# Group-norm attention on one core: the fp32 products for q and k in four column quarters of the array instead of two halves

## The chip, the cores and the metric

The kernel runs on one core of a Trainium2 chip. The metric is the device time of one launch in microseconds (us), lower is better. TensorE multiplies through a 128x128 array: a matmul holds a stationary operand (the weights; its rows are the contraction, its columns become output partitions in PSUM) and streams a moving operand of up to 512 columns past it. A matmul may use a part of the array only: 64 rows by 128 columns, 128 rows by 64 columns, and so on; matmuls on different parts can run beside each other. In the profile PE is the matmul side of TensorE and PEld its weight loads, DVE is VectorE, ACT ScalarE, POOL GpSimd, SP SyncE.

## The reference

```python
# x is (4, 512, 48, 48): b = 4 images, 512 channels, t = 2304 positions, 8 heads of d = 64
hn  = _group_norm(x, gn_scale, gn_bias)                       # 32 groups, fp32
qkv = einsum('oc,bchw->bohw', qkv_w, hn) + qkv_b              # fp32 product, 512 -> 1536 channels
qkv = qkv.reshape(b, 3, num_heads, d, t).astype(float16)
q, k, v = qkv[:, 0], qkv[:, 1], qkv[:, 2]
w = softmax(einsum('bhct,bhcs->bhts', q * scale, k * scale))
a = einsum('bhts,bhcs->bhct', w, v).astype(float32)
out = x + einsum('oc,bchw->bohw', proj_w, a) + proj_b
```

## The kernel before

The kernel has a fast path, which is what runs, and a fallback that a flag at the end would start. All sixteen pairs of heads (`g`, four in each image) go through the fast path one after the other. The positions are cut in five blocks (`QBLOCKS`, `j`): four of 512 and one of 256.

The work on TensorE has these parts. In brackets stand the part of the array that each uses, as rows x columns, and the line of the matmul:

- **scores** (64x128, L1134, tile `ps`): keys against queries in fp16, two heads at once, one in the upper and one in the lower 64 rows. ScalarE takes the exponential of the result (tile `p`, L1141).
- **values** (128x64, L1159, tile `av`): exponentials against v in fp16, one head in each 64 columns.
- **sums** (128x64, L1218, tile `sl`): exponentials against ones, at the end of each block.
- **v products** (128x64, L881, tile `pv`): normalised x against the v weights in fp32, two halves of 64 columns, 256 moving columns.
- **q and k products** (128x64, L829, tile `pqk`, in the opening `ps`, `first_av`, `first_w`): the q or k weights of a pair against normalised x in fp32, two halves of 64 columns, 512 or 256 moving columns. Each needs four channel chunks `c`, accumulated in one PSUM bank, which VectorE then empties into q or k (L840).
- **output projection** (128x128, L1019, tile `pr`).

The order on TensorE is fixed when the kernel is built. A list of steps (`stream`) has six to a block of 512 (three to the block of 256); a step issues the scores of three key tiles (or pairs of them), then fills in products that later pairs need, then the values of two steps before. `fill` takes those products from the list `beside`, in pieces: `chain_pieces` cuts a q or k chain of 512 columns in two pieces of two chunks each (`HALVES`) and leaves a chain of 256 whole. A step's pieces stand behind its values; in the step in which a block's sums are due, they stand between the sums and the values. The first 36 us hold the group norm of the first image with the first eight q and k chains. `idle_once` puts a no-op behind each of the first 190 matmuls of L829.

Of the kernel before, what the change touches and what calls it, by code (L numbers as in the profile page):

```python
# [23 lines left out]
HEADS, D = 8, 64  # L24
GROUP = C // 32
EPS = 1e-5
P = 128
# [448 lines left out]
def fast_path(  # L476
# [56 lines left out]
    wqkv = const.tile([P, NC, 3 * C], F32, name="wqkv")  # L533
# [93 lines left out]
    def chain_bank(name):  # L627
        if alone[0]:
            return ps_s.tile([P, 2, QB], F32, tag="ps", name=name)[:, 0, :]
        return ps_w.tile([P, QB], F32, tag="pw", name=name)  # L630
# [172 lines left out]
    def idle_once(*engines):  # L803
        for engine in engines:
            if idle_left[engine] > 0:
                idle_left[engine] -= 1
                getattr(nc, engine).nop("place", nofuse=True)
# [7 lines left out]
    def qk_steps(g, part, j, bank=None):  # L815
        b, pr = divmod(g, NPAIR)
        o, n = QBLOCKS[j]
        pw = {0: bank}

        def one(c):  # L820
            if g not in qk:
                qk[g] = [
                    qkp.tile([P, T], F16, tag=a, name=f"{a}_{g}") for a in ("q", "k")
                ]
            if c == 0 and bank is None:
                pw[0] = chain_bank(f"pqk_{g}_{part}_{j}")
            w0 = part * C + pr * P
            for lo in (0, D):
                nc.tensor.matmul(  # L829
                    pw[0][lo : lo + D, :n],  # L830
                    wqkv[:, c, w0 + lo : w0 + lo + D],
                    hn[b, c, j],
                    start=(c == 0),
                    stop=(c == NC - 1),
                )
                idle_once("tensor")

            def evacuate():
                col = part * NPAIR + pr
                nc.vector.tensor_scalar(  # L840
                    qk[g][part][:, o : o + n],
                    pw[0][:, :n],
                    bqkv[:, col : col + 1],
                    SCALE,
                    ALU.add,
                    ALU.mult,
                )

            if bank is not None:
                return evacuate  # L850
            if c == NC - 1:
                evacuate()

        return one
# [786 lines left out]
    n = QBLOCKS[j][1]  # L1641
# [141 lines left out]
```

## Time and profile before

| | before |
|---|---|
| median of 2 runs | 1588.49 us (1587.92 to 1589.07) |
| the profiled execution's own time | 1588.94 us |
| its span, first to last instruction | 1587.1 us |
| PE busy | 1572.5 us, 99% of the span |
| ACT busy | 1268.8 us, 80% |
| DVE busy | 1167.1 us, 74% |
| POOL busy | 319.3 us, 20% |
| mean granted TensorE clock | 0.998 |

The profile is of one execution. In a row of grouped instructions stand the line, the engine, the operation, what it writes and reads, the shapes and the count, then the busy time, the mean duration of one in ns and the idle time before them with what ended it. `128*64 128x512 f32` on a matmul is a stationary operand of 128 rows and 64 columns and a moving one of 512 columns. The ends of matmuls are modelled and overlap their successors, so the pace of TensorE is read from start to start. An fp32 matmul of the program shows as two weight loads and two matmuls in the trace; an fp16 one as one of each.

### The profile page before, as it was taken

To read this page: it belongs to the slowest core of one execution; us is meant where nothing else is said; L and a number is where in the kernel's file an instruction comes from. 1 tells how busy PE (TensorE), PEld (TensorE's weight loads), DVE (VectorE), ACT (ScalarE), POOL (GpSimd) and SP (SyncE) were. 2 spreads that over 40 slices of the span, in tenths; PEclk is the share of its full clock that TensorE was granted. 3 is DMA by queue.
4 is the path that set the end of the run, shared out by engine and by line. 5 is a ranking of instruction groups with operands and counts; after the bars stand their busy time and mean duration, and the time that the engine had idled before them with its cause. 6 is when DMAs were issued, how large, how long until landed. Compare 5 with 4: busy or idle time off the path is not lost. (4 is left out here: it accounts for less than half of the span.)

```text
span 1587.1 us, 28858 instructions
## 1 busy us (share of the span) xinstructions
PE 1572.5 (99%) x11526; PEld 678.0 (43%) x11526; DVE 1167.1 (74%) x1306; ACT 1268.8 (80%) x1363; POOL 319.3 (20%) x289
## 2 busy tenths in 40 slices
PE   9999999999999999999999999999999999999997
PEld 3733434443333543445333354344533334434543
DVE  6287678876766768987667766888767777777786
ACT  4177777888888888888888888888878888888995
POOL 1010201212212120311312231111122214131223
PEclk9999999999999999999999999999999999999999
DMA  7002120111212224621122222253022212215523
GB/s 226 1 21 78 48 75 27 31 57 48 68 42 63 68 58 121 170 81 42 51 67 57 56 63 68 85 173 101 12 67 64 68 48 65 68 48 175 163 70 128
DMA packets 115634, 119.87 MB, mean 76 GB/s; under 512 B 53156, under 2 KB 63268, under 8 KB 115492
## 3 DMA queue, kind: packets, MB, share of 16 engines
q1 hardware_dynamic: 113460, 116.11, 25.5%
q8 instruction: 92, 1.51, 0.4%
q10 hardware_dynamic: 1904, 1.84, 0.4%
q14 instruction: 50, 0.41, 0.1%
q0 software_dynamic: 128, 0.01, 0.0%
HBM read 79.58 MB, written 38.04 MB: 74 GB/s over the span
## 5 line engine op out<-in xcount | busy, mean ns | idle before, releaser
L1141 ACT ACTIVATE p<-ps 128x1024 f16<-128x1024 f32 x1296 | 1233.4, 1025 | 290.5 <-PE ps L1134 288.3
L1190 DVE TENSOR_TENSOR acc<-acc,p 128x3072 f16<-128x3072 f16 x270 | 495.7, 1836 | 51.9 <-ACT p L1141 49.4
L829 PE MATMUL pqk<-x,wqkv 128*64 128x512 f32 (+1 forms) x2432 | 510.3, 549 | 0.4 <-DVE k L840 0.3
L1159 PE MATMUL av<-p,v 128*64 128x512 f16 (+1 forms) x2880 | 360.7, 364 | 0.0
L1134 PE MATMUL ps<-q,k 64*128 64x512 f16 (+1 forms) x2880 | 356.1, 358 | 0.5 <-DVE v L889 0.2
L1286 POOL TENSOR_TENSOR att<-avx,ib 128x512 f16<-128x512 f32 (+1 forms) x78 | 123.1, 1578 | 1101.4 <-DMA ib<-row 835.3
L881 PE MATMUL pv<-wqkv,x 128*64 128x256 f32 x2304 | 267.6, 379 | 1.0 <-DVE v L889 1.0
L829 PEld LDWEIGHTS pqk<-x,wqkv 128*64 128x64 f32 x2432 | 168.6, 137 | 205.5 <-issue 155.8
L1134 PEld LDWEIGHTS <-k 64*128 64x128 f16 x2880 | 106.7, 94 | 287.8 <-issue 238.4
L1159 PEld LDWEIGHTS <-v 128*64 128x64 f16 x2880 | 131.4, 109 | 211.6 <-issue 167.0
L881 PEld LDWEIGHTS pv<-wqkv,x 128*64 128x64 f32 x2304 | 166.2, 137 | 82.5 <-DVE v L889 2.0
L1190 DVE TENSOR_TENSOR acc<-p,p 128x3072 f16<-128x3072 f16 x79 | 138.1, 1749 | 0.0
L1195 DVE TENSOR_TENSOR acc<-acc 128x1024 f16<-128x1024 f16 x156 | 134.7, 863 | 3.3
L953 POOL TENSOR_TENSOR pre<-pre,bproj 128x512 f32<-128x512 f32 x72 | 112.8, 1573 | 20.6 <-DMA pre<-x_dram 20.0
L889 DVE TENSOR_TENSOR v<-pv,bv 128x512 f16<-128x512 f32 x72 | 49.6, 690 | 77.7 <-PE pv L881 77.6
L840 DVE TENSOR_SCALAR q<-pqk,bqkv 128x512 f16<-128x512 f32 (+1 forms) x77 | 53.4, 693 | 70.9 <-PE pqk L829 70.6
L840 DVE TENSOR_SCALAR k<-pqk,bqkv 128x512 f16<-128x512 f32 (+1 forms) x75 | 52.1, 695 | 72.0 <-PE pqk L829 71.9
L1234 DVE COPY slx<-sl 128x512 f32<-128x512 f32 (+1 forms) x79 | 50.6, 641 | 62.4 <-PE sl L1218 62.4
L1019 PE MATMUL pr<-a,whi 128*128 128x512 f32 (+1 forms) x311 | 93.0, 418 | 0.0
L1041 DVE SCALAR_TENSOR_TENSOR r<-pr,r 128x512 f32<-128x512 f32 x75 | 51.5, 687 | 34.4 <-PE pr L1019 34.1
L1019 PE MATMUL pr<-att,wlo 128*128 128x512 f16 (+1 forms) x311 | 75.1, 361 | 0.6 <-DVE q L840 0.4
L1168 DVE COPY avx<-av 128x512 f32<-128x512 f32 (+1 forms) x79 | 50.4, 638 | 25.3 <-PE av L1159 25.2
(124 smaller groups left out, 456.5 us busy)
## 6 DMA issues: line engine op xcount, KB each, us to landing
pre<-x_dram SPq DMA_DIRECT2D x72, 256.0 KB, 3.1
xb<-pre SPq DMA_DIRECT2D x72, 256.0 KB, 3.3
r<-xb SPq DMA_DIRECT2D x72, 256.0 KB, 3.4
out_dram<-r SPq DMA_DIRECT2D x69, 256.0 KB, 2.6
ib<-row SPq DMA_DIRECT2D x126, 128.0 KB, 3.1
x<-x_dram SPq DMA_DIRECT2D x62, 256.0 KB, 4.2
x<-x_dram SPq DMA_DIRECT2D x16, 128.0 KB, 4.3
sums<-slx SPq DMA_DIRECT2D x128, 2.0 KB, 2.0
```

The source lines that it names most:

```text
L829: nc.tensor.matmul(pw[0][lo : lo + D, :n], wqkv[:, c, w0 + lo : w0 + lo + D], hn[b, c, j], start=(c == 0), stop=(c == NC - 1),)
L840: nc.vector.tensor_scalar(qk[g][part][:, o : o + n], pw[0][:, :n], bqkv[:, col : col + 1], SCALE, ALU.add, ALU.mult,)
L881: nc.tensor.matmul(pw[0][lo : lo + D, a, :], hn[b, c, i * P // QB][:, at + lo : at + lo + D], wqkv[:, c, 2 * C + half * C // 2 :][:, : C / ...
L953: nc.gpsimd.tensor_tensor(t, t, bias.to_broadcast(t.shape), ALU.add)
L1019: nc.tensor.matmul(ps[:, :n], w[:, bass.ts(m, P)], a, start=(i == 0), stop=(i == len(steps) - 1),)
L1041: nc.vector.scalar_tensor_tensor(xt, ps, DOWN, xt, ALU.mult, ALU.add)
L1134: nc.tensor.matmul(ps[:, h, a * n : (a + 1) * n], kt[rows, bass.ts(i, P)], qt[rows, o : o + n], start=True, stop=True,)
L1141: nc.scalar.activation(pt[:, r], ps, AF.Exp)
L1159: nc.tensor.matmul(av[0][lo : lo + D, :n], vv[b, pr // 2][:, i, pr % 2 * P + lo : pr % 2 * P + lo + D], pt[:, r, h, a * n : (a + 1) * n], ...
L1190: nc.vector.tensor_tensor(t, before, pt, ALU.add)
L1195: nc.vector.tensor_tensor(t[:, 0], t[:, 0], t[:, r], ALU.add)
L1286: nc.gpsimd.tensor_tensor(atts[g][:, o : o + n], avx.pop((g, j))[:, :n], ibs.pop((g, j))[:, :n], ALU.mult,)
```

## The change

Each q or k product of a chunk is now four matmuls of 32 columns, at the column positions 0, 32, 64 and 96, where it was two of 64. The sum over the chunks, the PSUM bank, the order of the pieces and all other engines' instructions stay as they are.

```diff
             w0 = part * C + pr * P
-            for lo in (0, D):
+            for lo in range(0, P, 32):
                 nc.tensor.matmul(
-                    pw[0][lo : lo + D, :n],
-                    wqkv[:, c, w0 + lo : w0 + lo + D],
+                    pw[0][lo : lo + 32, :n],
+                    wqkv[:, c, w0 + lo : w0 + lo + 32],
                     hn[b, c, j],
                     start=(c == 0),
                     stop=(c == NC - 1),
                 )
                 idle_once("tensor")
```

The first place is TensorE's order at an ordinary step of the first image: the values of an earlier step (`av`), half a q chain of the third pair (chunks 2 and 3, `x_2_1` and `x_3_1`), and the next scores. Of the program before:

```order
L1159 LDWEIGHTS v_0_517
L1159 MATMUL av_3_1504<-p_3_4_1552,v_0_517 64x512
L829 MATMUL pqk_0_1_1613<-x_2_1_129,wqkv 64x512 x2
L829 MATMUL pqk_0_1_1613<-x_3_1_139,wqkv 64x512 x2
L1134 LDWEIGHTS k_274
L1134 MATMUL ps_4_1_0_1662<-q_273,k_274 128x256
```

Of the changed program:

```order
L1159 LDWEIGHTS v_0_677
L1159 MATMUL av_3_1696<-p_3_4_1752,v_0_677 64x512
L829 MATMUL pqk_0_1_1821<-x_2_1_129,wqkv 32x512 x4
L829 MATMUL pqk_0_1_1821<-x_3_1_139,wqkv 32x512 x4
L1134 LDWEIGHTS k_274
L1134 MATMUL ps_4_1_0_1878<-q_273,k_274 128x256
```

Nothing moved; values and products were both 128x64 (written as 64 output partitions), and now a piece of 128x32 stands between the 128x64 values and the 64x128 scores. The second place is TensorE's order where a block ends: the sums (`sl`), half a q chain, then values. Of the program before:

```order
L1218 MATMUL sl_4_2915<-acc_4_2789,ones_160 64x256
L829 MATMUL pqk_0_3_2927<-x_0_3_111,wqkv 64x512 x2
L829 MATMUL pqk_0_3_2927<-x_1_3_123,wqkv 64x512 x2
L1159 LDWEIGHTS v_0_1854
L1159 MATMUL av_0_2933<-p_0_0_2824,v_0_1854 64x512
```

Of the changed program:

```order
L1218 MATMUL sl_4_3227<-acc_4_3093,ones_160 64x256
L829 MATMUL pqk_0_3_3239<-x_0_3_111,wqkv 32x512 x4
L829 MATMUL pqk_0_3_3239<-x_1_3_123,wqkv 32x512 x4
L1159 LDWEIGHTS v_0_2094
L1159 MATMUL av_0_3249<-p_0_0_3128,v_0_2094 64x512
```

Here, too, the order is the same, and the piece has 128x64 neighbours on both sides. Counted over the whole fast path, the neighbours of the q and k pieces on TensorE, the same in both programs, are:

| from | to | times | shape before | shape now |
|---|---|---|---|---|
| values | q/k | 198 | 64 to 64 columns | 64 to 32 |
| sums | q/k | 45 | 64 to 64 | 64 to 32 |
| q/k | values | 45 | 64 to 64 | 32 to 64 |
| q/k | v products | 1 | 64 to 64 | 32 to 64 |
| q/k | scores | 200 | 128x64 to 64x128 | 128x32 to 64x128 |
| scores | q/k | 2 | 64x128 to 128x64 | 64x128 to 128x32 |

TensorE changes the shape of the array part 954 times in the program before and 1243 times in the changed one. The matmuls of L829 go from 1280 to 2560, 4 of 5 with 512 moving columns and the rest with 256.

## The prediction

> **What bounds the kernel now.** I read the page first: its first line, the busy time of TensorE, and the strip of its busy tenths.
>
> ```profile
> span 1587.1 us, 28858 instructions
> PE 1572.5 (99%) x11526; PEld 678.0 (43%) x11526; DVE 1167.1 (74%) x1306; ACT 1268.8 (80%) x1363; POOL 319.3 (20%) x289
> PE   9999999999999999999999999999999999999997
> ```
>
> A busy 99% proves little on its own, because matmul ends are modelled. So I asked next what PE waited for; the columns are the total, the number of times and the longest wait in us.
>
> ```profile
> engine line waited for: us in total, times, longest us
> PE count L1722 <- DVE good L1721: 2.5, 1, 2.5
> PE idle L1482 <- DVE busy L1478: 1.5, 1, 1.5
> PE pv L881 <- DVE v L889: 1.0, 2, 0.9
> ```
>
> The two longest are the closing count and the opening; between them PE waits for about 1 us in all. TensorE is the bound from end to end, ScalarE and VectorE have a fifth and a quarter of the span to spare, and whatever TensorE gains or loses in the long middle reaches the end one for one. So the question is what a q or k piece costs on TensorE: its streaming, and its joints with the work before and behind it.
>
> **Streaming.** The first view is the timeline of PE at the end of a block, columns: start, length, engine, line, operation, names, shapes, count.
>
> ```profile
> 226.30 0.82 PE L1134 MATMUL ps<-q,k 64*128 64x512 f16 x6
> 227.05 0.41 PE L1218 MATMUL sl<-acc,ones 128*64 128x512 f16 x2
> 227.29 1.88 PE L829 MATMUL pqk<-x,wqkv 128*64 128x512 f32 x8
> 229.01 0.81 PE L1159 MATMUL av<-p,v 128*64 128x512 f16 x6
> 229.75 0.82 PE L1134 MATMUL ps<-q,k 64*128 64x512 f16 x6
> ```
>
> The lengths overlap; the pace is in the starts. The piece of two chunks has 8 records and hands over after 229.01 - 227.29 = 1.72 us. Records run in pairs, one in each half of the columns, so these are 4 rounds of **0.43 us**. An fp16 round of 512 takes half of that: the six values, three rounds, with a joint of 0.10 behind them (below), take 229.75 - 229.01 = 0.74, so (0.74 - 0.10) / 3 = 0.21. A 256-column fp32 round has its row here:
>
> ```profile
> 234.41 1.89 PE L829 MATMUL pqk<-x,wqkv 128*64 128x256 f32 x16
> 236.24 0.82 PE L1134 MATMUL ps<-q,k 64*128 64x512 f16 x6
> ```
>
> (1.83 - 0.10) / 8 rounds = 0.216 us. How many rounds there are follows from the counts of the line:
>
> ```profile
> L829 PE MATMUL pqk<-x,wqkv x2432: 379/592/643, 36.7 to 1440.1; 128*64 128x512 f32 x150, 128*64 128x256 f32 x38
> L829 PE MATMUL ps<-x,wqkv x96: 379/592/643, 10.7 to 34.6; 128*64 128x512 f32 x80, 128*64 128x256 f32 x16
> L829 PE MATMUL first_av<-x,wqkv x16: 592/592/593, 15.6 to 35.4; 128*64 128x512 f32 x16
> L829 PE MATMUL first_w<-x,wqkv x16: 592/592/593, 16.5 to 36.3; 128*64 128x512 f32 x16
> ```
>
> 2432 + 96 + 16 + 16 = 2560 records, two for each of the program's 1280 matmuls, are 1280 rounds, 1024 of 0.43 and 256 of 0.216: 440 + 55 = **495 us** of streaming on this line. Cut in quarters, a chunk has 4 matmuls with 2 records each. If all four quarters run at once, these are 2 rounds, as many as the halves need now, and a round streams the same 512 columns. The change removes nothing: it puts 4 x 32 columns where 2 x 64 filled the same 128. I take the streaming at no change. The bounds are wide, since no row shows four parts at work: if only two quarters ran at once, the rounds double, +495 us; if the two-fold length of an fp32 round came from the two halves hindering each other and vanished with narrow parts, a round could fall to the fp16 0.21, about -247 us. I choose nothing because the nearest rows, pairs of fp16 and of fp32 halves, each keep one steady pace.
>
> The added records must also be issued. With 256 columns a quartered round is 4 loads and 4 matmuls in 0.216 us, 27 ns each. The scores of the short block already run so:
>
> ```profile
> 161.85 0.83 PE L1134 MATMUL ps<-q,k 64*128 64x256 f16 x12
> 162.61 0.84 PE L1159 MATMUL av<-p,v 128*64 128x512 f16 x6
> ```
>
> 12 matmuls and as many loads in 0.76 - 0.10 = 0.66 us are 27 ns each, without a gap. So issue costs nothing; the no-ops that now end after half as many products fall away with it.
>
> **The joints.** Here the timeline of PE shows an ordinary step, and two steps in which the output projection follows the values:
>
> ```profile
> 215.62 0.84 PE L1159 MATMUL av<-p,v 128*64 128x512 f16 x6
> 216.29 1.88 PE L829 MATMUL pqk<-x,wqkv 128*64 128x512 f32 x8
> 218.10 0.82 PE L1134 MATMUL ps<-q,k 64*128 64x512 f16 x6
> ...
> 630.29 0.84 PE L1159 MATMUL av<-p,v 128*64 128x512 f16 x6
> 631.07 1.04 PE L1019 MATMUL pr<-att,wlo 128*128 128x512 f16 x4
> ...
> 633.72 0.84 PE L1159 MATMUL av<-p,v 128*64 128x512 f16 x6
> 634.49 1.04 PE L1019 MATMUL pr<-att,wlo 128*128 128x512 f16 x4
> ```
>
> The same six values, entered from scores each time, hand over to q/k after 0.67 us, and to the projection after 0.78 and 0.77. The products keep the shape 128x64; the projection goes to 128x128, with the rows unchanged. So a change of the columns alone costs **0.10 us**. The way out to the scores costs the same: 218.10 - 216.29 = 1.81 against the 1.72 of the block's end, where values of the same shape follow.
>
> A second, smaller price falls on the first round behind a change, since its weights can't be loaded under the work before. The six values take 0.74 to the scores at 229.01, where they follow products of their shape; entered from scores, with a joint behind, they take 0.77 (above): 0.03. For fp32 weights of 64 columns a row exists too:
>
> ```profile
> 76.84 1.94 PE L829 MATMUL pqk<-x,wqkv 128*64 128x512 f32 x8
> 78.71 1.11 PE L1134 MATMUL ps<-q,k 64*128 64x512 f16 x6
> ```
>
> This piece was entered from scores and takes 1.87, not 1.81: 0.06. No row has fp32 weights of 32 columns. They are half as wide, so I take half, 0.03; the bounds are 0 and 0.06. Four quarters that start one after another may cost something too. This row shows how an offset is paid:
>
> ```profile
> 104.58 0.85 PE L1159 MATMUL av<-p,v 128*64 128x512 f16 x6
> 105.37 0.82 PE L1134 MATMUL ps<-q,k 64*128 64x512 f16 x6
> ```
>
> Here six values behind a product take 0.79 instead of 0.74, because the two halves run apart until the next change of shape; 0.05 is my upper bound for that in an entry, and I take nothing.
>
> **The sum.** The order on TensorE gives 198 + 45 = 243 entries into a q/k piece from 128x64 work and 45 + 1 = 46 ways out into it; all 289 were free and become changes of shape. The 200 ways out to scores and the 2 entries from them are changes now and stay so. Each new one costs 0.10 and a first load of 0.03 (32 fp32 columns on the way in, 64 fp16 columns on the way out): 289 x 0.13 = **+37.6 us**. Against the profiled execution's 1588.94 (its span of 1587.1 and 1.8 around it; the median, 1588.49, is 0.03% lower) that is 1626.5. The lower bound leaves the joint alone, 289 x 0.10 = 28.9, so 1617.8; the upper takes 243 x (0.10 + 0.06 + 0.05) + 46 x 0.13 = 57.0, so 1646. Nothing on another engine hides this: VectorE and ScalarE wait for TensorE, and a longer TensorE only lengthens their waits. A longer run also moves no order, since that is fixed.
>
> **The rivals.**
>
> *No change of shape between 64 and 32 columns* (the other side). The 0.10 is seen where columns go from 64 to 128. If two column widths can follow each other without emptying the array, 289 times nothing remains, 1589, or up to 1596 with first loads in 243 entries at 0.03. It decides at 31.8 us (2%) over 289, or 0.11 us a joint: below, the kernel is not slower by over 2%. Against it: every change of shape in the rows, of rows or of columns, costs about 0.10. Chance 0.10.
>
> *Two quarters at a time.* The rounds double: 1588.9 + 37.6 + 495 = 2122. For it: nothing in this trace has more than two parts working at once. Against it: two parts keep their pace whatever they stream. Chance 0.08.
>
> *Four at once, but slower.* Four fp32 streams read twice what any row here reads at a time; if a round stretches, each per cent costs 5 us on top of 1626.5, anything from 1646 to 2122. Chance 0.07. The Trainium skill, in "TensorE: Matmul & The Clock Gate" (Measured speedup vs the span model), has three column tiles of 512 columns at 2.38 times, not 3. Taken as a rate, rounds would stretch by 3 / 2.38 = 1.26, an estimate of 1755 us. The halves here show no such loss, and nothing in this trace shows three or more.
>
> *A faster round.* If narrow parts run an fp32 round at the fp16 pace, 495 falls by 247: 1588.9 + 37.6 - 247 = 1379. For it, only that 0.43 is twice 0.21; against it, both records of a matmul take 0.43 steadily, with two streams of equal width to the fp16 case. Chance 0.04. The Trainium skill, "TensorEngine Tiling (Array Packing)" (Theoretical Speedup), gives up to 2 times for 64 and up to 4 times for 32 columns, which read as a promise is this rival. It speaks of a matrix that is small, and here four small ones make up the same 128 columns.
>
> That the change isn't in effect is no rival: the order shows 2560 matmuls of 32 columns.
>
> **How the numbers follow.** My forecast, four quarters at the old pace with 289 new changes of shape, has 0.71, and its own range is 1618 to 1646. To hold 8 in 10 the range takes in the case without a price for the change: 1589 to 1646, 0.81. Over 2% (about what a measurement of this kernel can tell from no change) begins at 1620.3. The forecast lies above it unless a joint costs under 0.11, which I give 0.10 of its 0.71. Slower: 0.61 + 0.08 + 0.07 = 0.76; within 2%: 0.10 + 0.10 = 0.20; faster: 0.04.
>
> **What would show it.** In the timeline of the changed kernel the starts from values to a q/k piece should lie 0.77 us apart, not 0.67; a two-chunk piece of 16 records should reach the scores after about 1.84, and from the sums to it there should be 0.34, not 0.24. If the first is 0.67, the joint is free; if the piece takes 3.5, only two run at once; if it takes 1.0, rounds got shorter. PE should still wait for about nobody, and ScalarE's idle time should grow by what the span does.

## The result, and the profile after

The changed kernel takes 1627.53 us (median of 2 runs, 1627.44 to 1627.62) against 1588.49 before: 1.0246 times as long, 95% interval 1.0202 to 1.029, or +39.0 us. The profiled execution took 1627.44 us with a span of 1625.6.

The head of its page, and the longest waits of PE (total us, times, longest):

```profile
span 1625.6 us, 33978 instructions
PE 1610.0 (99%) x14086; PEld 645.4 (40%) x14086; DVE 1167.4 (72%) x1306; ACT 1268.9 (78%) x1363; POOL 323.7 (20%) x289
```

```profile
PE count L1722 <- DVE good L1721: 2.5, 1, 2.5
PE idle L1482 <- DVE busy L1478: 1.5, 1, 1.5
PE first_means L729 <- DVE moments L655: 1.3, 1, 1.3
PE pv L881 <- DVE v L889: 1.0, 2, 0.9
```

The matmul records grew by 2560, the span by 38.5 us, and PE still waits for almost nobody. The 1.3 us at `first_means` lie in the opening, and the opening is no longer for it: the first q and k chain starts at 10.41 us, where it started at 10.74. VectorE and ScalarE have the same busy times as before; the exponentials' idle time went from 290.5 to 328.8 us in this group of the page, +38.3, which is the span's growth handed on. Before and after:

```profile
L1141 ACT ACTIVATE p<-ps 128x1024 f16<-128x1024 f32 x1296 | 1233.4, 1025 | 290.5 <-PE ps L1134 288.3
L1141 ACT ACTIVATE p<-ps 128x1024 f16<-128x1024 f32 x1296 | 1233.5, 1025 | 328.8 <-PE ps L1134 324.6
```

The timeline of PE in the changed kernel (start, length, engine, line, operation, names, shapes, count), first ordinary steps, then the end of a block:

```profile
219.50 0.84 PE L1159 MATMUL av<-p,v 128*64 128x512 f16 x6
220.27 1.93 PE L829 MATMUL pqk<-x,wqkv 128*32 128x512 f32 x16
222.12 0.82 PE L1134 MATMUL ps<-q,k 64*128 64x512 f16 x6
...
227.02 3.64 PE L829 MATMUL pqk<-x,wqkv 128*32 128x512 f32 x32
230.59 0.82 PE L1134 MATMUL ps<-q,k 64*128 64x512 f16 x6
231.35 0.41 PE L1218 MATMUL sl<-acc,ones 128*64 128x512 f16 x2
231.68 1.92 PE L829 MATMUL pqk<-x,wqkv 128*32 128x512 f32 x16
233.54 0.84 PE L1159 MATMUL av<-p,v 128*64 128x512 f16 x6
234.31 0.82 PE L1134 MATMUL ps<-q,k 64*128 64x512 f16 x6
```

Values to q/k: 220.27 - 219.50 = **0.77**, where it was 0.67. Sums to q/k: 0.33, where it was 0.24. The piece to the scores: 222.12 - 220.27 = 1.85, where it was 1.81. The piece to the values: 233.54 - 231.68 = 1.86, where it was 1.72. These values to the scores: 0.77, where it was 0.74. The longer piece of four chunks takes 230.59 - 227.02 = 3.57, 1.72 more than the one of two. So two more chunks, four rounds, still take 4 x 0.43 us: the streaming is as it was, and all of the loss lies at the edges of the pieces. The steps shown are typical: all 180 places where six values of 512 columns hand over to q/k have 0.76 to 0.77 now, and had 0.67 to 0.68 before.

The 0.04 by which a piece grew can be taken apart by its rounds. These rows are from narrow windows of the timeline, first of the changed kernel's piece at 220.27, then of the piece at 216.29 in the kernel before; `x1` is the last record of the last round:

```profile
220.27 0.64 PE L829 MATMUL pqk<-x,wqkv 128*32 128x512 f32 x4
220.72 0.61 PE L829 MATMUL pqk<-x,wqkv 128*32 128x512 f32 x4
...
221.58 0.61 PE L829 MATMUL pqk<-x,wqkv 128*32 128x512 f32 x4
221.60 0.59 PE L829 MATMUL pqk<-x,wqkv 128*32 128x512 f32 x1
222.12 0.39 PE L1134 MATMUL ps<-q,k 64*128 64x512 f16 x2
```

```profile
216.29 0.59 PE L829 MATMUL pqk<-x,wqkv 128*64 128x512 f32 x2
216.72 0.59 PE L829 MATMUL pqk<-x,wqkv 128*64 128x512 f32 x2
...
217.57 0.59 PE L829 MATMUL pqk<-x,wqkv 128*64 128x512 f32 x2
217.58 0.59 PE L829 MATMUL pqk<-x,wqkv 128*64 128x512 f32 x1
218.10 0.39 PE L1134 MATMUL ps<-q,k 64*128 64x512 f16 x2
```

The first round takes 220.72 - 220.27 = 0.45, where it took 0.43: about 0.02 for the first load. The fourth quarter of a round starts 0.02 behind the first, where the two halves start 0.01 apart at most: about 0.02 for the quarters' starts one after another. From the start of the last record to the scores, both kernels take 0.52.

From these rows an entry costs 0.10 + 0.04 (1.85 against 1.81) and a way out to values 0.10 + 0.03: 243 x 0.14 + 46 x 0.13 = 40.0 us, against 39.0 measured and 38.5 in the spans; each row is rounded to 0.01.

### The profile page after: what moved, and what is told of

It reads as the page before. It is cut to its first block, busy times and chain, and to the rows that moved or that the text cites. A ratio compares the mean times of both kernels' runs of the same rounds, so it can differ in the third digit from the quotient of the medians.

```text
span 1625.6 us, 33978 instructions
## 1 busy us (share of the span) xinstructions
PE 1610.0 (99%) x14086; PEld 645.4 (40%) x14086; DVE 1167.4 (72%) x1306; ACT 1268.9 (78%) x1363; POOL 323.7 (20%) x289
## 5 line engine op out<-in xcount | busy, mean ns | idle before, releaser
L1141 ACT ACTIVATE p<-ps 128x1024 f16<-128x1024 f32 x1296 | 1233.5, 1025 | 328.8 <-PE ps L1134 324.6
L829 PE MATMUL pqk<-x,wqkv 128*32 128x512 f32 (+1 forms) x4864 | 520.1, 554 | 0.2
L829 PEld LDWEIGHTS pqk<-x,wqkv 128*32 128x32 f32 x4864 | 135.5, 109 | 263.6 <-issue 230.0
L1159 PEld LDWEIGHTS <-v 128*64 128x64 f16 x2880 | 127.3, 109 | 223.0 <-issue 179.6
L881 PEld LDWEIGHTS pv<-wqkv,x 128*64 128x64 f32 x2304 | 161.4, 137 | 87.8 <-DVE v L889 2.8
```

The costliest lines, as they stand in the source:

```text
L829: nc.tensor.matmul(pw[0][lo : lo + 32, :n], wqkv[:, c, w0 + lo : w0 + lo + 32], hn[b, c, j], start=(c == 0), stop=(c == NC - 1),)
L881: nc.tensor.matmul(pw[0][lo : lo + D, a, :], hn[b, c, i * P // QB][:, at + lo : at + lo + D], wqkv[:, c, 2 * C + half * C // 2 :][:, : C / ...
L1141: nc.scalar.activation(pt[:, r], ps, AF.Exp)
L1159: nc.tensor.matmul(av[0][lo : lo + D, :n], vv[b, pr // 2][:, i, pr % 2 * P + lo : pr % 2 * P + lo + D], pt[:, r, h, a * n : (a + 1) * n], ...
```

## The experiments

Two theories stood against each other. The first: a change of the array part's shape between one matmul and the next costs TensorE about 0.10 us, plus the first load of weights, and the quarters made 289 such changes out of free joints. The second: the quarters are dear in themselves, by twice the matmuls and weight loads to issue or by slower streaming of narrow parts. The second could give the same total, since 39 us over 1280 added matmuls is only 30 ns each. The factors ("times") below are against runs of the kernel before on the same chip as the experiment. Their median is 1589.13 us for twice the records, all in quarters, v in quarters too and the whole array, and 1588.92 for the repeat of all in quarters, k in quarters and the mirror.

**Twice the records, no new change of shape.** The kernel before with this in `qk_steps`:

```diff
-            for lo in (0, D):
+            todo = [(c, slice(0, n))]
+            if bank is None and n == QB:
+                cut = bass.ts(c // 2, n // 2)
+                todo = [(2 * (c % 2), cut), (2 * (c % 2) + 1, cut)]
+            for cc, cut in todo:
+                for lo in (0, D):
...
```

> The kernel before, with its halves of 64 columns, but each q/k chain of 512 moving columns streams them in two parts of 256: as many matmuls and weight loads for those chains as the quarters have, and no new change of shape (954, as before). Theory (the changes of shape cost): only the two shorter rounds for each longer one, 1024 times 2 x 0.216 - 0.43, about +2 to +4 us, so about 1592. Rival (the doubled records cost, by issue or by weight loads): about what the quarters cost, 1625 or more.

1590.81 us (10 runs), 1.0012 times, interval 1.0003 to 1.0022: +1.7 us. The timeline of PE:

```profile
215.47 0.84 PE L1164 MATMUL av<-p,v 128*64 128x512 f16 x6
216.15 1.89 PE L834 MATMUL pqk<-x,wqkv 128*64 128x256 f32 x16
217.97 0.82 PE L1139 MATMUL ps<-q,k 64*128 64x512 f16 x6
```

16 records now stand where the kernel before has 8, as with the quarters, and the starts are 0.68 and 1.82 apart, against 0.67 and 1.81 there. Over the whole kernel PE has 13462 records instead of 11526: 1936 more, not quite the 2560 of the quarters, since the opening and the chains of 256 are left whole. At 39 us for 2560 they would have cost about 29 us, and they cost 1.7. The rival of records falls.

**All in quarters.** The changed kernel with v, values and sums cut in the same way:

```diff
# v_chain
-                for lo in (0, D):
+                for lo in range(0, P, 32):
...
# values
-                for h in range(2):
-                    lo = h * D
+                for lo in range(0, P, 32):
+                    h = lo // D
                     nc.tensor.matmul(
-                        av[0][lo : lo + D, :n],
-                        vv[b, pr // 2][:, i, pr % 2 * P + lo : pr % 2 * P + lo + D],
+                        av[0][lo : lo + 32, :n],
+                        vv[b, pr // 2][:, i, pr % 2 * P + lo : pr % 2 * P + lo + 32],
...
# add_up: the same loop, with ones16[:, :32]
```

> Quarters for all that was 128x64: q/k, v, values and sums. All 289 new joints are between equal shapes again (954 changes of shape, as before). Theory (it is the mismatch with the neighbours that costs): values to q/k takes about 0.67 us again where the block has 512 columns. In the blocks of 256 the values need 8 records in 0.108 us, 13.5 ns each, twice the pace that any row shows; if 27 ns is the limit, their 288 rounds and some 50 of the sums take 0.216, +36 us. So 1589 to 1625 by that, all of an excess in the short blocks. Rival (quarters cost by themselves): above the 1627.5 of the changed kernel, and values to q/k at 0.77 still.

1586.78 us (10 runs), 0.9984 times, interval 0.9974 to 0.9993. With the most matmuls of all (19504 records) it is 41 us faster than the changed kernel (0.9984 against 1.0246 times the kernel before), whose quarters it has. The timeline of PE in an ordinary step, then in a short block:

```profile
215.20 0.83 PE L1159 MATMUL av<-p,v 128*32 128x512 f16 x12
215.85 1.89 PE L829 MATMUL pqk<-x,wqkv 128*32 128x512 f32 x16
217.68 0.82 PE L1134 MATMUL ps<-q,k 64*128 64x512 f16 x6
```

```profile
173.94 0.84 PE L1159 MATMUL av<-p,v 128*32 128x256 f16 x24
174.61 1.89 PE L829 MATMUL pqk<-x,wqkv 128*32 128x512 f32 x16
```

Values to q/k is 0.65, the piece 1.83. So the quarters themselves are free where their neighbours have quarters too, and the rival of slow quarters falls. The expected excess in the short blocks is not there: 24 matmuls and as many loads pass in 0.67 us, 14 ns each, where the kernel before takes 0.68 for the same values in halves, so 27 ns was only the most that earlier rows had asked for.

The same kernel was timed again, since its first timing was a little under the kernel before:

> The kernel with all in quarters once more, timed in more rounds, because its first timing lay 0.16% under the kernel before. Theory: the first round of values and sums behind scores is 0.226 and not 0.240 us, 428 times 0.014 = -6 us, against some 0.007 for the later start of the third and fourth quarter at up to 430 ways out, +3 us: 0.998 times the kernel before. Rival (that was noise of the first timing): 1.000.

1587.48 us (11 runs), 0.9991 times, interval 0.9982 to 1.0. The gain of 1.4 to 2.4 us is at the edge of what the timing resolves, and its size is left open; at the least, this version is no slower than halves all round.

**v in quarters too.** The changed kernel, with this in `v_chain` and nothing else:

```diff
-                for lo in (0, D):
+                for lo in range(0, P, 32):
                     nc.tensor.matmul(
-                        pw[0][lo : lo + D, a, :],
-                        hn[b, c, i * P // QB][:, at + lo : at + lo + D],
+                        pw[0][lo : lo + 32, a, :],
+                        hn[b, c, i * P // QB][:, at + lo : at + lo + 32],
```

> The changed kernel with the v products in quarters as well: 112 more entries from values or sums, 22 more ways out to values, one joint between q/k and v gone: 133 more changes of shape (1376). Theory: at the 0.135 us each that the changed kernel paid (39.0 over 289), +18 us on the changed kernel, 1645.5, and 1.036 times the kernel before. Rival (a cost of the q/k line itself, not of joints): v has 9 parts in 10 as many records as q/k and streams 256 columns, so a cost by record would add about 35 us, 1662; no cost of joints would leave 1627.

1643.88 us, 1.0344 times, interval 1.0327 to 1.0362: +54.7 us on the kernel before, so about 16 on the changed kernel for 133 more changes of shape, 0.12 each. The interval holds the expected 1.036; the rival's 1662 us would be 1.046 and lies outside. The timeline of PE at a v piece:

```profile
205.01 0.84 PE L1159 MATMUL av<-p,v 128*64 128x512 f16 x6
205.78 1.93 PE L881 MATMUL pv<-wqkv,x 128*32 128x256 f32 x32
```

Values to v is 0.77 here, as values to q/k is.

**The whole array.** The kernel before, one matmul to a chunk:

```diff
-            for lo in (0, D):
-                nc.tensor.matmul(
-                    pw[0][lo : lo + D, :n],
-                    wqkv[:, c, w0 + lo : w0 + lo + D],
+            nc.tensor.matmul(
+                pw[0][:, :n],
+                wqkv[:, c, w0 : w0 + P],
...
```

> The kernel before with each q/k chunk as one matmul of 128 columns: half the records, but the same 288 joints now lie between 64 and 128 columns (1242 changes of shape). Theory: 0.10 a joint, and a first load of 128 fp32 columns, about twice the 0.05 to 0.06 that 64 columns showed: 243 x 0.21 + 45 x 0.13 = +57 us, about 1645. A piece of two chunks then has 4 records, one at a time; that it still streams in 1.72 is the test of whether a record takes 0.43 us by itself. Rival (two halves hinder each other): a record falls to 0.21 and the time to about 1400. Rival (more or narrower records cost, not joints): no slower than before.

1641.91 us, 1.0331 times, interval 1.0314 to 1.0349: +52.8 us, with half the records in this line. The timeline of PE:

```profile
216.70 3.70 PE L828 MATMUL pqk<-x,wqkv 128*128 128x512 f32 x8
220.33 0.82 PE L1133 MATMUL ps<-q,k 64*128 64x512 f16 x6
...
224.52 0.84 PE L1158 MATMUL av<-p,v 128*64 128x512 f16 x6
225.29 1.98 PE L828 MATMUL pqk<-x,wqkv 128*128 128x512 f32 x4
227.21 0.82 PE L1133 MATMUL ps<-q,k 64*128 64x512 f16 x6
```

Values to q/k is 0.77 again, now towards the wider shape. The piece takes 1.92: its four records run one at a time, 4 x 0.43 = 1.72, with the 0.10 of the way out and 0.10 for the first load of 128 columns. The piece of four chunks needs no such sum: it takes 220.33 - 216.70 = 3.63, so four more records, with the same edges, take 1.71. So a record of 512 fp32 columns takes 0.43 us by itself, and the rival that halves hinder one another falls. The forecast of 57 was a little high: the wide load is 0.10, not 0.11.

**k in quarters, q in halves.** In `qk_steps` of the kernel before:

```diff
-            for lo in (0, D):
+            wide = 32 if part == 1 else D
+            for lo in range(0, P, wide):
...
```

> Quarters for the k products, halves for q. The order has 150 new changes of shape (1104), 120 entries and 30 ways out, instead of the 289 of the changed kernel. Theory: 0.135 us each as there, 150 x 0.135 = +20 us on the kernel before, 1609. A cost of the quarters' streaming or of their records would be half of 39, also about +20, so this run tells only whether the price goes by the count.

1608.35 us, 1.0122 times, interval 1.0106 to 1.0137: +19.4 us for 150 changes, 0.13 each. The total alone could also be half of a cost of the quarters' records; the timeline of PE tells them apart, with a q piece in halves first and a k piece in quarters behind it:

```profile
218.66 0.84 PE L1160 MATMUL av<-p,v 128*64 128x512 f16 x6
219.33 1.88 PE L830 MATMUL pqk<-x,wqkv 128*64 128x512 f32 x8
...
225.13 0.84 PE L1160 MATMUL av<-p,v 128*64 128x512 f16 x6
225.90 3.64 PE L830 MATMUL pqk<-x,wqkv 128*32 128x512 f32 x32
```

In one run the values hand over after 0.67 us to halves and after 0.77 us to quarters. The price is paid joint by joint.

**The mirror.** The kernel before with values and sums in quarters, q/k and v in halves; in `values`, and alike in `add_up`:

```diff
-                for h in range(2):
-                    lo = h * D
+                for lo in range(0, P, 32):
+                    h = lo // D
                     nc.tensor.matmul(
-                        av[0][lo : lo + D, :n],
+                        av[0][lo : lo + 32, :n],
...
```

> The mirror: values and sums, in fp16, in quarters; q/k and v stay in halves. 355 entries into q/k and v from values or sums and 67 ways back become changes of shape (1376). The q/k records are those of the kernel before. Theory (the mismatch costs, whoever has the narrow part): 355 x (0.10 + 0.05, a first load of 64 fp32 columns) + 67 x 0.11, less 0.014 on 428 first loads of values and sums that are half as wide: 53 + 7 - 6 = +54 us, about 1643. Rival (narrow fp32 products cost by themselves): no slower than the kernel before.

1645.19 us, 1.0355 times, interval 1.0339 to 1.0371: +56.3 us. The timeline of PE:

```profile
220.63 0.83 PE L1159 MATMUL av<-p,v 128*32 128x512 f16 x12
221.39 1.94 PE L829 MATMUL pqk<-x,wqkv 128*64 128x512 f32 x8
223.26 0.82 PE L1134 MATMUL ps<-q,k 64*128 64x512 f16 x6
```

Values to q/k is 0.76, though the q/k piece is word for word that of the kernel before, and the piece takes 1.87, the 0.06 of a first load of 64 fp32 columns that the kernel before shows behind scores. The joint costs its 0.10 whichever side is narrow.

## Why the prediction was right, point by point

- **The bound.** TensorE's loss came through one for one: 38.5 us in the span, 38.3 in the exponentials' idle time. The "about 1 us" of other waits was read a little low: beside the 1.0 us for v, the list of the kernel before has seven shorter waits of 2.0 us in all. It made no difference.
- **Streaming at no change.** Right, and now seen: two more chunks in four quarters take 1.72. The whole-array run adds that a record takes its 0.43 us alone, so nothing was to be gained from narrower parts.
- **Issue at no cost.** Right, and with room: 14 ns a record pass where 27 were argued from.
- **The joint, 0.10.** Right, though it was carried over from joints of 64 to 128 columns: 0.77 against 0.67 at the entries, 1.86 against 1.72 at the ways out, first load included.
- **The first load, 0.03 on the way in.** The pieces grew by 0.04, and not by the load alone. The first round is about 0.02 longer, a little less than the 0.03. The other 0.02 is the later start of the fourth quarter, a term that the forecast named and put at nothing. The two misses partly cancel, which is luck, if small.
- **The sum.** 37.6 us forecast, 39.0 measured. The 0.01 that is missing at each entry makes 243 x 0.01 = 2.4 us, and the rounding of the rows leaves the rest.
- **The range.** 1589 to 1646 was wide enough to hold a kernel that pays nothing for a joint, so a time inside it shows little by itself. The 0.77, the 1.72 and the runs above carry the mechanism.
- **The rivals.** No price between 64 and 32 columns: out by the 0.77. Two at a time, or four but slower: out by the 1.72. A faster round: out by the same row. The figure for three column tiles in the Trainium skill, "TensorE: Matmul & The Clock Gate" (Measured speedup vs the span model), taken as a rate, would have given 1755, an estimate. Four quarters here stream without loss, 1.72 us for four rounds.

What the 0.10 consists of stayed open. The rows show it between 64 and 32 columns, between 64 and 128, and on the way to the scores, where the rows change too, but nothing inside it, and no run took it apart.

## What to carry to other kernels

Where TensorE is the bound and its work is interleaved in short pieces, the shape of the array part belongs to the order of the work: a piece that differs from its neighbours pays at each edge. In this kernel a new edge cost 0.13 us between 32 and 64 columns, whichever side was the narrow one (39.0 us over 289, 56.3 over 422 in the mirror), and 0.18 between 64 and 128 columns (52.8 over 288), where the first load is longer. Cut all the matmuls that stand beside each other to one shape, or none; count the changes of shape in the order and multiply before trying. Narrower column parts brought no speed for products that fill 128 columns anyway.

## What the runs showed of the hardware that was not expected

- Loads and matmuls of 32-column parts pass at 14 ns a record (24 of each in 0.67 us), half of the 27 ns at which the scores of the short block pass.
- Four quarters do not start quite together behind a change of shape: the fourth starts 0.02 us after the first, and a piece takes that much longer.
- Quarters can be a shade better than halves where the neighbours agree: the step shown has 0.65 from values to q/k where halves have 0.67. In time it is 0.9984 and 0.9991 in two timings, too little to claim a size.
